# A four-layer graph, mixture and expert network on one core: the edge check moved into the mixture, node scaling into the counting, and a ring of fifteen weight tiles in the last stage

## The chip, the core and the metric

The kernel runs on 1 core of one Trainium2 chip. TensorE multiplies matrices, VectorE, ScalarE and GpSimd compute on its results, and SyncE issues most loads; 16 DMA engines move the data. The metric is device time in microseconds (us); the number that counts is the median of several executions. A profile is one further execution.

## The reference, cut to what matters

512 nodes of 768 features pass through four layers; each adds to the nodes x a graph network over 8704 edges, a linear-attention mixture, and a feed-forward stage with or without experts. Order: gnn0/mix0, ffn0, mix1/gnn1, ffn1, mix2/gnn2, ffn2, mix3/gnn3, ffn3.

```python
edge_index = jnp.stack([src, dst])
xn = _layernorm(x, axis=-1)
x = x + _L0_gnn_ref(xn, edge_index, edge_attr_256, ...)  + _L0_mix_ref(xn[None], ...)[0]
x = x + _L0_ffn_ref(_layernorm(x, axis=-1)[None], ...)[0]
...
x = x + _L3_ffn_ref(_layernorm(x, axis=-1)[None], ...)[0]
```

The last stage, 16 experts of which each takes the 64 nodes that score highest for it:

```python
scores = jax.nn.sigmoid(x @ gate_weight.T)
topk_score, topk_ids = jax.lax.top_k(scores.T, capacity)   # capacity 64
xg = x[topk_ids]
gate = jax.nn.silu(jnp.einsum('ecd,efd->ecf', xg, Wg))
up = jnp.einsum('ecd,efd->ecf', xg, Wu)
out = jnp.einsum('ecf,edf->ecd', gate * up, Wd) * topk_score[..., None]
y = jnp.zeros((n, d), x.dtype).at[topk_ids.reshape(-1)].add(out.reshape(-1, d))
shared = jax.nn.silu(hidden_states @ Ws_g.T) * (hidden_states @ Ws_u.T) @ Ws_d.T
```

## The kernel before, in words

Nodes lie as 4 blocks of 128 (NT = 4), features as 6 chunks of 128 (KC = 6). A scheduler orders instructions by the program's order and the tiles' readers and writers; `issue_after` holds an instruction behind another. Memory of a pool that is closed goes to the next one, which then waits for the old tiles' last users.

**Counting (`counts`, first 237 us).** Edges become one-hot rows (`ohd`, `so`), and matmuls (L516) count edges per pair of nodes for three or four types, packed as digits of one number. L474 sums the edge features. `digits` (L476) takes each of four blocks apart: ScalarE casts the bytes to S and R (L488, L490), GpSimd and VectorE add them up (L493 to L498) with totals kept in `total`, and GpSimd stores them. L533 to L544 then compare the totals with what they must be: a sum over VectorE (L535), a matmul with ones, and the flag `big`. If the flag is set, `counts_any` counts in another way; the test stands at L2089 (load of the flag) and L2090 (branch), behind mix0. gnn2 (L1560) loads the flag again. Nodes are normalized (`norm`) into xn, which lies where the counting's tiles lay; so its scaling (L406) waits for the end of the counting. `to_fm` turns xn into xnT by 24 transposes (L355) and six copies (L250, L252). Then mix0 starts with its v blocks (L334).

**Gates of ffn0 and ffn2 (`moe`).** The gate's weight wg is loaded on ScalarE's queue at the start of `moe`.

**End of the third mixture.** Its last projection adds the 8 blocks of 512 x 768 to x; beside it runs the rest of gnn3, whose last add to x is L1796. Each block of x that is done is normalized and stored to `there` by GpSimd (L1704). `to_fm` with `cut` turns three of four blocks early.

**Last stage (`ffn3`).** Experts go in pairs q = 0 to 7, hidden features in 8 parts n of 384: 64 steps. A step needs 4 tiles of weights up (two experts, Wg and Wu) and 2 tiles down (Wd), each 128 x 2304 floats, 1152 KB, loaded by SyncE (L258) into a ring (pool `f3_w`) of 13. The ring's pool is opened after `self.cw.close()`, so its memory holds everything that the earlier stages' weights (`wp`, 6 tiles) and bias rows (`rowp`) held, and more. At any time the up of step i + 1 (L1981) is issued ahead of the down of step i (L1997).

The start, in order: gate matmuls (L342), scores sc (L1850), then `first_rank` (L1858) for experts 0 and 1: transposes put all scores of an expert on every partition, in one bank of PSUM; per block of nodes ScalarE counts by signs (L1865), VectorE settles ties (L1868). `choose` builds one-hot rows oh (L1896), `fetch` multiplies them with the node numbers, casts `who` (L1909) and gathers the chosen rows from HBM on GpSimd's queue (L1911). `turn` transposes the rows to xg, which the first up needs. Twelve units of a shared expert (`shared`, `shared_down`, weights `sw` loaded by GpSimd, L1950, ring of 6) fill gaps by a list `beside` written per step; unit 0's two up halves stand around the first fetch. `rank` for later pairs, `way` (weights back to nodes) and `back` (adds to x) are in `beside` too.

Of the kernel before, what the change touches and what calls it, by code (L numbers as in the profile page):

```python
# [10 lines left out]
F32 = mybir.dt.float32  # L11
# [159 lines left out]
class Net:  # L171
    def __init__(self, ctx, tc, dram, at, out):
        self.tc, self.nc, self.d, self.at, self.out = tc, tc.nc, dram, at, out
        nc = self.nc
        self.cw = ExitStack()
        self.wp = self.cw.enter_context(tc.tile_pool(name="wp", bufs=6, side="right"))
        self.keep = ctx.enter_context(tc.tile_pool(name="keep", bufs=1))
        self.small = ctx.enter_context(tc.tile_pool(name="small", bufs=4))
        self.rowp = self.cw.enter_context(tc.tile_pool(name="rowp", bufs=2, side="right"))
# [87 lines left out]
    def wk(self, ap):  # L267

        return self.w(ap).rearrange("p (k n) -> p k n", k=KC)
# [87 lines left out]
    def to_fm(self, x, out, cut=0):  # L357

        if cut:
            ps = [self.ps() for _ in range(KC)]  # L360
            for t in range(cut // P):
                for f in range(KC):
                    self.tr(ps[f][:, t * P : (t + 1) * P], x[:, t, f * P : (f + 1) * P])
            for f in range(KC):
                self.copy(out[:, f, :cut], ps[f][:, :cut])
            for f in range(0, KC, 3):
                p = self.ps()
                for k in range(3):
                    self.tr(p[:, k * P : (k + 1) * P], x[:, NT - 1, (f + k) * P : (f + k + 1) * P])
                self.copy(out[:, f : f + 3, cut:], p[:, :HW].rearrange("p (k n) -> p k n", k=3))  # L370
            return
        ps = [self.ps() for _ in range(KC)]
        for t in range(NT):
            for f in range(KC):
                self.tr(ps[f][:, t * P : (t + 1) * P], x[:, t, f * P : (f + 1) * P])
        for f in range(KC):
            self.copy(out[:, f, :], ps[f])

# [16 lines left out]
    def norm1(self, x, out, t):  # L395

        nc = self.nc
        st = self.small.tile([P, 2, 6], F32, name="st")
        mv = self.small.tile([P, 2], F32, name="mv")
        r = self.small.tile([P, 1], F32, name="rs")  # L400
        for h in range(2):
            nc.vector.bn_stats(st[:, h, :], x[:, t, h * HW : (h + 1) * HW])
        nc.vector.bn_aggr(mv, st)
        self.root = nc.scalar.activation(r, mv[:, 1:2], AF.Sqrt, bias=self.eps).ins
        nc.vector.reciprocal(r, r)
        nc.vector.tensor_scalar(out[:, t, :], x[:, t, :], mv[:, 0:1], r, OP.subtract, OP.mult)  # L406
# [24 lines left out]
    def counts(self, c0, g0):  # L431
# [11 lines left out]
        after = c0.enter_context(tc.tile_pool(name="g0_t", bufs=1))  # L443
        EFT = after.tile([P, 2, N], F32, name="EFT")
        with ExitStack() as c:
# [11 lines left out]
            top = one.tile([P, 8], F32, name="top")  # L457
            total = one.tile([P, 10], F32, name="total")
# [20 lines left out]
            def digits(h, t, ps):  # L479
# [9 lines left out]
                R = dg.tile([P, 3, N], F32, name="R", bufs=1)  # L489
# [3 lines left out]
                nc.gpsimd.tensor_add(A, R[:, 0, :], R[:, 1, :])  # L493
# [12 lines left out]
            for h in range(2):  # L506
# [15 lines left out]
                for t in range(2):  # L522
                    digits(h, t, [acc[t, n] for n in range(2)])

                while len(left) > (17, 0)[h]:
                    features(left.pop(0))
            for f in range(2):
                self.copy(EFT[:, f, :], eft[f])

            three = one.tile([P, EJ], F32, name="three")  # L530
            nc.vector.tensor_scalar(three, ind[:, 3, :], 2.0, None, OP.is_le, OP.add, accum_out=total[:, 8:9])
            nc.vector.tensor_scalar(total[:, 8:9], total[:, 8:9], -1.0, float(-EJ), OP.mult, OP.add)
            nc.vector.memset(total[:, 9:10], 0.0)  # L533
            check = one.tile([P, 2], F32, name="check")
            nc.vector.tensor_reduce(check[:, 0:1], total, AX.X, OP.add)  # L535
            high = one.tile([P, 1], F32, name="high")
# [4 lines left out]
            bad = one.tile([P, 2], F32, name="bad")  # L541
# [3 lines left out]
        return AT, EFT, after  # L545
# [98 lines left out]
    def mix0(self, xnT):  # L644
# [3 lines left out]
        with ExitStack() as outer, ExitStack() as c:  # L648
# [16 lines left out]
            self.tm(d["m0_wqkv"], xs, put_v, self.bias(d["m0_bv"]), nbs=(4, 5), bias_at=2 * D)  # L665
            for g in range(2):
                qk = one.tile([97, 2, 4, N], F32, name="qk")
# [49 lines left out]
            self.project(outer, attn, "m0")  # L717
# [97 lines left out]
    def moe(self, f, act, xn, xnT, bs=None, fill=None, later=None):  # L815
# [6 lines left out]
        with ExitStack() as c:  # L822
            one = c.enter_context(tc.tile_pool(name=f + "_one", bufs=1))
            two = c.enter_context(tc.tile_pool(name=f + "_two", bufs=2))
            wg = one.tile([P, KC, 32], F32, name="wg")
            nc.scalar.dma_start(wg.rearrange("p k e -> p (k e)"), d[f + "_wg"])
# [732 lines left out]
    def gnn2(self, xn, xnT):  # L1559
        big = self.nc.values_load(self.big[:1], min_val=0, max_val=1)  # L1560
        with self.tc.If(big > 0) as cmp:
# [252 lines left out]
    def ffn3(self, xnT, gate, there):  # L1814
# [5 lines left out]
        with ExitStack() as c:  # L1820
            two = c.enter_context(tc.tile_pool(name="f3_two", bufs=2))
            one = c.enter_context(tc.tile_pool(name="f3_one", bufs=1))
            sp = c.enter_context(tc.tile_pool(name="f3_s", bufs=6))

            self.cw.close()
            self.wp = c.enter_context(tc.tile_pool(name="f3_w", bufs=13))

            first = self.small.tile([P, 1], F32, name="r3")
            with self.tc.issue_after(self.root):
                nc.scalar.activation(first, self.eps, AF.Sigmoid)  # L1830
            io = one.tile([P, P], F32, name="io")
            nc.gpsimd.iota(io, pattern=[[1, P]], base=0, channel_multiplier=0, allow_small_or_imprecise_dtypes=True)
            number = self.number
            above = one.tile([P, NT, NX], F32, name="above")
            counted = one.tile([P, NX, NT, 3], F32, name="counted")
# [5 lines left out]
            side = one.tile([P, 7 * P], BF16, name="side")  # L1841
# [4 lines left out]
            loT = one.tile([P, N], F32, name="loT")  # L1846
# [12 lines left out]
            def first_rank(e):  # L1859
                p = self.ps()  # L1860
                for t in range(NT):
                    self.tr(p[:, t * P : (t + 1) * P], sc[:, t, e : e + 1].to_broadcast([P, P]))
                for t in range(NT):
                    junk = one.tile([P, N], BF16, name="sign")
                    i = nc.scalar.activation(junk, p, AF.Sign, scale=BIGGER, bias=low[:, t, e : e + 1],  # L1865
                                             accum_out=signs[:, t, e : e + 1])
                    junk = one.tile([P, N], BF16, name="junk")
                    nc.vector.scalar_tensor_tensor(junk, p, sc[:, t, e : e + 1], side[:, (3 - t) * P : (7 - t) * P],  # L1868
                                                   OP.is_equal, OP.mult, accum_out=sides[:, t, e : e + 1])
                return i  # L1870

            def rank(e):
# [4 lines left out]
                for t in range(NT):  # L1877
                    s = sc[:, t, e : e + 1]
                    for n, (a, b, op) in enumerate(((0, t * P, OP.is_ge), (t * P, N, OP.is_gt))):
                        if a < b:  # L1880
                            junk = one.tile([P, N], BF16, name="junk")
                            nc.vector.tensor_scalar(junk[:, a:b], p[:, a:b], s, None, op, OP.add,
                                                    accum_out=counted[:, e, t, n : n + 1])
                    junk = one.tile([P, N], BF16, name="junk")
                    nc.vector.scalar_tensor_tensor(junk[:, :P], p[:, t * P : (t + 1) * P], s, before, OP.is_equal, OP.mult,
                                                   accum_out=counted[:, e, t, 2:3])
                nc.vector.tensor_reduce(above[:, :, e : e + 1], counted[:, e], AX.X, OP.add)
# [3 lines left out]
            def choose(q):  # L1891

                oh = two.tile([P, NT, 2, CAP], BF16, name="oh")
                chosen[q] = oh, two.tile([P, KC, P], F32, name="xg")
# [4 lines left out]
            rows = {}  # L1899

            def fetch(q):
# [4 lines left out]
                sums = two.tile([P, 1], F32, name="sums")  # L1906
                nc.vector.tensor_reduce(sums, p[:, :2], AX.X, OP.add)
                who = two.tile([P, 1], I32, name="who")
                nc.vector.tensor_copy(who, sums)  # L1909
                rows[q] = two.tile([P, D], F32, name="rows", bufs=1)  # L1910
                nc.gpsimd.indirect_dma_start(out=rows[q], out_offset=None, in_=there,  # L1911
                                             in_offset=bass.IndirectOffsetOnAxis(ap=who, axis=0))
                return i
# [10 lines left out]
            def way(q):  # L1924

                oh = chosen[q][0]
                os = two.tile([P, NT, 2, CAP], F32, name="os", bufs=1)
                nc.vector.tensor_mul(os, oh, sc[:, :, 2 * q : 2 * q + 2, None].to_broadcast([P, NT, 2, CAP]))
                ways[q] = two.tile([P, N], F32, name="ohT")
# [15 lines left out]
            def shared(u, b):  # L1945
                if b == 0:
                    hs[u] = [two.tile([P, N], F32, name="hs")]
# [6 lines left out]
                i = self.acc(p, [(w[:, k, :], xnT[:, k, :]) for k in range(KC)])  # L1954
                h = hs[u][0]
                if b == 0:
# [12 lines left out]
            def up_w(q, n):  # L1969
                return [[self.wk(d[w][2 * q + a, n]) for a in range(2)] for w in ("f3_Wg", "f3_Wu")]  # L1970

            def down_w(q, n):
                return [self.wr(d["f3_Wd"][2 * q + a, n]) for a in range(2)]

            def up(q, n, ws):
# [7 lines left out]
                h = two.tile([P, HW], F32, name="h")  # L1983
# [4 lines left out]
            def down(q, n, h, wd, po):  # L1988
# [3 lines left out]
                hT = two.tile([P, HW], F32, name="hT")  # L1992
# [18 lines left out]
            for q in range(8):  # L2011
                beside[8 * q + 2].append((way, q))
# [8 lines left out]
            rest = pieces[2:]  # L2021
# [3 lines left out]
            for e in range(2):  # L2025
                last = first_rank(e)
            nc.vector.tensor_scalar(signs, signs, 0.5, float(N // 2), OP.mult, OP.add)
            nc.vector.tensor_add(above[:, :, :2], signs, sides)
            with tc.issue_after(last.ins):
                last = shared(0, 0)  # L2030
            choose(0)

            with tc.issue_after(last.ins):
                last = fetch(0)
            with tc.issue_after(last.ins):
                shared(0, 1)
            turn(0)
            held = up(*steps[0], up_w(*steps[0]))
            for i, (q, n) in enumerate(steps):
# [9 lines left out]
                if n == 7:  # L2049
                    outs[q] = two.tile([P, D], F32, name="outs")  # L2050
# [11 lines left out]
def tile_net(ctx, tc, dram, at, out, only=ALL):  # L2062
# [10 lines left out]
    with ExitStack() as ck, ExitStack() as c0:  # L2073
        g0 = c0.enter_context(tc.tile_pool(name="g0", bufs=1))
        if "counts" in only:
            AT, EFT, g0_t = net.counts(c0, g0)
# [82 lines left out]
```

## Time and profile before

| | us |
|---|---|
| median of 3 executions (4174.07 to 4178.53) | 4176.57 |
| profiled execution | 4179.75 |
| its span | 4177.7 |
| TensorE busy in the span | 4027.0 (96%) |
| VectorE, ScalarE, GpSimd busy | 1214.8, 648.5, 274.4 |
| DMA moved | 710.89 MB, mean 170 GB/s |
| ring weights of the last stage | 384 loads of 1152.0 KB, 22.2 from issue to landing |
| mean granted TensorE clock | 0.989 |

Rows of the profile give an engine, the line of the code, the operation, output and inputs by the program's names, and a count; idle time of the engine just ahead stands in brackets, with what ended it. PEld is TensorE's loading of weights. The slices divide the span in 40 equal parts of 104 us; digits are tenths busy. A wait is given as the engine and line waiting, what it waited for, the time in total, how often, and the longest.

### The profile page before, as it was taken

Reading aid. Unit: us, or ns where it says so; the run is one execution under the profiler, and the core shown is the slowest. Engines: PE = TensorE matmul, PEld = TensorE weight load, DVE = VectorE, ACT = ScalarE, POOL = GpSimd, SP = SyncE. Lnnn points to the kernel's source line nnn. Section 1 sums busy time; section 2 is a strip of 40 time slices with the busy share of each in tenths; the row PEclk is TensorE's granted clock in tenths of the full one; section 3 lists DMA queues with packets and bytes.
Section 4 is the critical chain, followed back from the end, with each engine's and each line's share of the span. In section 5 each row is a group of like instructions: output and inputs, shape, how many; then the busy total and the mean of one; then the engine's idle time right before and its main releaser. Section 6 shows DMA issues by size and latency. Waiting matters only on the chain. (4 is left out here: it accounts for less than half of the span.)

```text
span 4177.7 us, 39229 instructions
## 1 busy us (share of the span) xinstructions
PE 4027.0 (96%) x16020; PEld 2066.7 (49%) x16061; DVE 1214.8 (29%) x2899; ACT 648.5 (16%) x1222; POOL 274.4 (7%) x329
## 2 busy tenths in 40 slices
PE   8989999999999999999999999999989999999998
PEld 3444555554455667655544444454644444444443
DVE  7721211113332147313411111126832122212211
ACT  1212000012222216311101010024510000000000
POOL 1120000010031010000000000020200000000000
PEclk9999999999999999999999999999999999999999
DMA  3210011121184011302211111082099999999998
GB/s 124 71 69 34 35 63 51 53 78 36 62 312 143 23 70 46 132 25 78 98 46 57 46 61 42 3 325 82 15 373 422 421 421 421 421 422 421 422 422 361
DMA packets 99548, 710.89 MB, mean 170 GB/s; under 512 B 12608, under 2 KB 12944, under 8 KB 29984
## 3 DMA queue, kind: packets, MB, share of 16 engines
q1 hardware_dynamic: 78064, 601.20, 36.0%
q0 software_dynamic: 16816, 95.80, 6.1%
q10 hardware_dynamic: 4480, 11.28, 0.7%
q8 instruction: 131, 2.15, 0.2%
q14 instruction: 57, 0.47, 0.0%
HBM read 685.68 MB, written 22.54 MB: 170 GB/s over the span
## 5 line engine op out<-in xcount | busy, mean ns | idle before, releaser
L1981 PE MATMUL ps<-w,xg 128*64 128x384 f32 x3072 | 567.6, 489 | 5.3 <-DMA w<-in_f_Wg_dram 3.0
L1981 PEld LDWEIGHTS ps<-w,xg 128*64 128x64 f32 x3072 | 235.3, 137 | 293.1 <-issue 264.1
L1601 PE MATMUL ps<-aT,w 128*128 128x512 f32 x864 | 372.3, 592 | 0.0
L1997 PE MATMUL ps<-w,hT 128*64 128x384 f32 x1536 | 322.5, 490 | 6.3 <-DMA w<-in_f_Wd_dram 2.9
L334 PE MATMUL ps<-xnT,w 128*128 128x512 f32 (+1 forms) x732 | 322.8, 598 | 0.2 <-ACT xnT L252 0.2
L1601 PEld LDWEIGHTS ps<-aT,w 128*128 128x128 f32 x864 | 164.2, 190 | 203.6 <-issue 202.3
L334 PE MATMUL ps<-w,xnT 128*128 128x384 f32 x672 | 222.7, 488 | 0.0
L334 PEld LDWEIGHTS ps<-xnT,w 128*128 128x128 f32 (+1 forms) x732 | 134.7, 185 | 176.3 <-issue 172.7
L1997 PEld LDWEIGHTS ps<-w,hT 128*64 128x64 f32 x1536 | 132.5, 136 | 171.8 <-issue 146.5
L411 DVE TENSOR_TENSOR x<-x,ps 128x384 f32<-128x384 f32 x224 | 123.4, 553 | 263.7 <-PE ps L334 193.0
L334 PE MATMUL ps<-C,parts 128*128 128x512 bf16 x843 | 187.8, 380 | 3.5 <-DVE inv L1623 2.4
L334 PE MATMUL ps<-w,hT 128*128 128x384 f32 x552 | 184.6, 490 | 2.6 <-ACTq L1056 1.7
L334 PEld LDWEIGHTS ps<-w,xnT 128*128 128x128 f32 x672 | 127.7, 191 | 88.8 <-issue 5.8
L1611 DVE TENSOR_TENSOR aT<-inv,ps 128x512 f32<-128x512 f32 x72 | 49.4, 686 | 365.7 <-PE ps L334 365.7
L1984 ACT ACTIVATE h<-ps 128x384 f32<-128x384 f32 x64 | 31.4, 490 | 788.9 <-PE ps L1981 788.9
L516 PE MATMUL ps<-ohd,so 128*128 128x512 bf16 x533 | 128.4, 391 | 21.1 <-DVE so L513 20.4
L1985 DVE TENSOR_TENSOR h<-h,ps 128x384 f32<-128x384 f32 x64 | 35.4, 554 | 376.8 <-PE ps L1981 376.8
L334 PEld LDWEIGHTS ps<-w,hT 128*128 128x128 f32 x552 | 103.1, 190 | 80.1 <-ACT xbT L252 7.1
L334 PE MATMUL ps<-w,aT 128*128 128x384 f32 (+1 forms) x416 | 139.6, 486 | 0.5 <-DVE aT L250 0.4
L334 PE MATMUL ps<-xnT,sw 128*128 128x512 f32 x288 | 139.6, 616 | 0.0
L334 PEld LDWEIGHTS <-parts 128*128 128x128 bf16 x864 | 84.8, 98 | 108.1 <-issue 8.9
L334 PE MATMUL ps<-w,nodesT 128*128 128x384 f32 x384 | 129.1, 486 | 0.0
(507 smaller groups left out, 4634.7 us busy)
## 6 DMA issues: line engine op xcount, KB each, us to landing
w<-in_f_Wg_dram SPq DMA_DIRECT2D x128, 1152.0 KB, 22.2
w<-in_f_Wu_dram SPq DMA_DIRECT2D x128, 1152.0 KB, 22.2
w<-in_f_Wd_dram SPq DMA_DIRECT2D x128, 1152.0 KB, 22.2
w<-in_g_w_dram SPq DMA_DIRECT2D x54, 1152.0 KB, 5.2
w<-in_m_wqkv_dram SPq DMA_DIRECT2D x24, 1152.0 KB, 7.5
w<-in_g_t_dram SPq DMA_DIRECT2D x12, 1152.0 KB, 5.1
w<-in_m_wp_dram SPq DMA_DIRECT2D x8, 1152.0 KB, 5.1
ea<-in_edge_attr_dram SPq DMA_DIRECT2D x34, 256.0 KB, 2.7
```

The source lines that it names most:

```text
L334: i = self.nc.tensor.matmul(out, a, b, start=n == 0, stop=n == len(pairs) - 1)
L411: self.nc.vector.tensor_add(xs, xs, p)
L516: nc.tensor.matmul(p, so[:, n, t * P : (t + 1) * P], ohd[:, j, :], start=j == 0, stop=j == EJ - 1)
L1601: nc.tensor.matmul(outs[nb * 3 + f], w[:, k, f * P : (f + 1) * P], xT[:, k, :], start=first and k == 0, stop=last and k == KC - 1)
L1611: nc.vector.tensor_mul(aT[:, f, :], inv[:, r, :], p)
L1981: nc.tensor.matmul(p[a * 64 : a * 64 + 64, :HW], xg[:, k, a * CAP : (a + 1) * CAP], ws[b][a][:, k, :], start=k == 0, stop=k == KC - 1)
L1984: nc.scalar.activation(h, pg[:, :HW], AF.Silu)
L1985: nc.vector.tensor_mul(h, h, pu[:, :HW])
L1997: nc.tensor.matmul(po[nb][a * 64 : a * 64 + 64, :HW], hT[:, f * P + a * 64 : f * P + a * 64 + 64], wd[a][:, f, nb * HW : (nb + 1) * HW], s ...
```

## The change

- **Counting.** Small totals lie in a tile of their own for the whole kernel (`edge`). xn gets memory on the other side of the pools, and `norm` is called inside the counting. The check becomes a function `checked`, called in mix0 behind the v blocks; the flag is loaded once, ahead of mix0's second group (`self.wrong`), for both tests. R is kept in BF16. Some bias loads are held behind the first half's adds (`self.after`).
- **Gates.** `gate_of` loads the gate weights on GpSimd's queue into the caller's pool.
- **`to_fm_last`** replaces `to_fm` with `cut`: which engine copies what is fixed; the sigmoid's table load stands behind the last copy.
- **ffn3.** The ring has 15 tiles: six of `wp` (indices 0 to 3, 9, 10), five of `early`, two of `tail`, two of `rest_`, in the places of earlier tiles, so that each waits for its own place. All tiles of the ring start on multiples of 512 bytes. Several tiles are single-buffered or share a tag (`outs`, `os`, `h`, hT, hs, ohT); sw has 5 buffers. `first_ranks` uses two banks: ScalarE works on one expert while VectorE works on the other. `who` is cast by the reduction. shared(0, 1) is split around the first fetch, and `shared_down` of unit 0 comes ahead of the rows' transposes.

```diff
-    def to_fm(self, x, out, cut=0):
...
+    def gate_of(self, pool, f):
+        t = pool.tile([P, KC, 32], F32, name=f + "_gate")
+        self.nc.gpsimd.dma_start(t.rearrange("p k e -> p (k e)"), self.d[f])
+        return t
...
+    def to_fm_last(self, x, out):
+
+        nc, cut = self.nc, (NT - 1) * P
+        ps = [self.ps() for _ in range(KC)]
+        for t in range(NT - 1):
+            for f in range(KC):
+                self.tr(ps[f][:, t * P : (t + 1) * P], x[:, t, f * P : (f + 1) * P])
+        for f in (0, 1, 3, 4):
+            i = nc.scalar.copy(out[:, f, :cut], ps[f][:, :cut])
+        with self.tc.issue_after(self.scaled):
+            for f in (2, 5):
+                nc.vector.tensor_copy(out[:, f, :cut], ps[f][:, :cut])
...
-                R = dg.tile([P, 3, N], F32, name="R", bufs=1)
+
+                R = dg.tile([P, 3, N], BF16, name="R", bufs=1)
...
+        def checked():
+
             nc.vector.tensor_reduce(check[:, 0:1], total, AX.X, OP.add)
-            high = one.tile([P, 1], F32, name="high")
             nc.vector.tensor_reduce(high, top, AX.X, OP.max)
             nc.vector.tensor_scalar(check[:, 1:2], high, 2.0 ** 24, None, OP.is_ge)
             p = self.ps()
             self.acc(p[:, :2], [(self.ones, check)])
-            bad = one.tile([P, 2], F32, name="bad")
             nc.vector.tensor_scalar(bad, p[:, :2], 0.0, None, OP.not_equal)
...
-            self.tm(d["m0_wqkv"], xs, put_v, self.bias(d["m0_bv"]), nbs=(4, 5), bias_at=2 * D)
+            with tc.issue_after(self.after):
+                bv = self.bias(d["m0_bv"])
+            self.tm(d["m0_wqkv"], xs, put_v, bv, nbs=(4, 5), bias_at=2 * D)
+            checked()
             for g in range(2):
+                if g:
+                    self.wrong = nc.values_load(self.big[:1], min_val=0, max_val=1)
...
-            wg = one.tile([P, KC, 32], F32, name="wg")
-            nc.scalar.dma_start(wg.rearrange("p k e -> p (k e)"), d[f + "_wg"])
...
-            sp = c.enter_context(tc.tile_pool(name="f3_s", bufs=6))
-
-            self.cw.close()
-            self.wp = c.enter_context(tc.tile_pool(name="f3_w", bufs=13))
+            tail = c.enter_context(tc.tile_pool(name="f3_m", bufs=2))
+            sp = c.enter_context(tc.tile_pool(name="f3_s", bufs=5))
+            c.callback(self.cw.close)
+            early = c.enter_context(tc.tile_pool(name="f3_w", bufs=5))
+            self.cr.close()
+            rest_ = c.enter_context(tc.tile_pool(name="f3_r", bufs=2))
+            self.taken = 0
+
+            def ring():
+                i, self.taken = self.taken % 15, self.taken + 1
+                return self.wp if i < 4 or 9 <= i < 11 else early if i < 9 else tail if i < 13 else rest_
...
+            def first_ranks():
+
+                ps = [self.ps() for _ in range(2)]
+                for e in range(2):
+                    for t in range(NT):
+                        self.tr(ps[e][:, t * P : (t + 1) * P], sc[:, t, e : e + 1].to_broadcast([P, P]))
+                for e in range(2):
+                    for t in range(NT):
+                        junk = two.tile([P, N], BF16, tag="h", name="sign")
+                        i = nc.scalar.activation(junk, ps[e], AF.Sign, scale=BIGGER, bias=low[:, t, e : e + 1],
+                                                 accum_out=signs[:, t, e : e + 1])
+                    for t in range(NT):
+                        junk = one.tile([P, N], BF16, name="junk")
+                        j = nc.vector.scalar_tensor_tensor(
+                            junk, ps[1 - e], sc[:, t, 1 - e : 2 - e], side[:, (3 - t) * P : (7 - t) * P],
+                            OP.is_equal, OP.mult, accum_out=sides[:, t, 1 - e : 2 - e])
+                return i, j
...
-                hT = two.tile([P, HW], F32, name="hT")
+                hT = two.tile([P, HW], F32, name="hT", bufs=1)
...
-            rest = pieces[2:]
+            rest = pieces[4:]
...
+            last, _ = first_ranks()
             nc.vector.tensor_scalar(signs, signs, 0.5, float(N // 2), OP.mult, OP.add)
             nc.vector.tensor_add(above[:, :, :2], signs, sides)
+
             with tc.issue_after(last.ins):
                 last = shared(0, 0)
             choose(0)
-
             with tc.issue_after(last.ins):
-                last = fetch(0)
+                last = shared(0, 1, lambda: fetch(0))
             with tc.issue_after(last.ins):
-                shared(0, 1)
+                for t in range(NT):
+                    shared_down(0, t)
             turn(0)
...
         if "counts" in only:
-            AT, EFT, g0_t = net.counts(c0, g0)
...
+            right = ExitStack()
+            xn = right.enter_context(tc.tile_pool(name="L0n", bufs=1, side="right")).tile([P, NT, D], F32, name="xn")
+            AT, EFT, g0_t, checked = net.counts(c0, g0)
+            with tc.issue_after(net.begun[0]), tc.issue_after(net.begun[1]):
+                net.constants()
+                net.norm(net.x, xn)
...
-                wrong = nc.values_load(net.big[:1], min_val=0, max_val=1)
-                with tc.If(wrong > 0):
+                with tc.If(net.wrong > 0):
```

## The prediction on record

> **What bounds the kernel now.** I read the slices of the span first, then a table by stage, then the timeline of the two places where TensorE stands still, and last the waits and the chain.
>
> ```profile
> PE   8989999999999999999999999999989999999998
> DMA  3210011121184011302211111082099999999998
> GB/s 124 71 69 34 35 63 51 53 78 36 62 312 143 23 70 46 132 25 78 98 46 57 46 61 42 3 325 82 15 373 422 421 421 421 421 422 421 422 422 361
> ```
>
> TensorE is busy nearly everywhere, so time falls only where it pauses or where it waits for bytes. DMA is at nine tenths in the last eleven slices alone: that is the last stage (ffn3). The slice before it moves almost nothing (15 GB/s). By stage (PE, PEld, DVE, ACT, POOL busy, granted clock, DMA share, GB/s):
>
> ```profile
> 2950.00:3000.00 50.00, 49.83 (x265) 34.30 (x264) 46.96 (x78) 30.17 (x48) 15.56 (x11) 1.00 0.00 1
> 3000.00:3050.00 50.00, 48.36 (x239) 32.70 (x238) 29.11 (x64) 15.37 (x27) 10.69 (x20) 1.00 0.31 110
> 3050.00:3100.00 50.00, 40.33 (x185) 18.80 (x185) 18.23 (x59) 10.16 (x23) 2.15 (x3) 0.90 1.01 418
> 3100.00:3200.00 100.00, 99.26 (x512) 44.34 (x512) 19.25 (x53) 5.97 (x13) 3.17 (x5) 1.00 1.01 421
> ```
>
> The DMA engines idle until 3043.68, when the first ring weight is issued, and are then full. The queue's own waits say why: ring issues (L258) stand behind the release of the whole area.
>
> ```profile
> SPq L258 <- DVE x L1796: 128.0, 1, 128.0
> ```
>
> From 3043.68 to the last landing at 4164.03 the stream runs 1120.35 us without a pause; 384 weight tiles go by in pairs 5.57 us apart (2.787 each). The chain ends on it, so near its end the stage is bound by bytes:
>
> ```profile
> 4141.79 22.19 DMA w<-in_f_Wd_dram
> 4163.98 0.04 issue
> 4164.03 4.08 PE ps L1997 x20
> ```
>
> But all of TensorE's waits for weights come in 4124–4164 and sum to only about 8 us. Both limits lie close together: that caps what earlier loads can bring.
>
> TensorE's own pauses at the start of that stage, and in front of the first mixture:
>
> ```profile
> 3043.45 2.13 PE L355 MATMUL ps<-ident,xn 128*128 128x128 f32 x18
> 3052.80 5.32 PE L334 MATMUL ps<-xnT,sw 128*128 128x512 f32 x12
> 3065.43 0.75 PE L334 MATMUL ps<-number,oh 128*128 128x2 bf16 x4 [7.31 <-issue]
> 3066.04 8.20 PE L334 MATMUL ps<-xnT,sw 128*128 128x512 f32 x12
> 3075.92 2.48 PE L1981 MATMUL ps<-w,xg 128*64 128x384 f32 x14 [0.32 <-DVE xg L250]
> ```
>
> ```profile
> 245.25 0.56 PE L334 MATMUL ps<-check,ones 128*128 128x2 f32 x2 [7.81 <-DVE check L535]
> 246.42 2.52 DVE L406 TENSOR_SCALAR xn<-x,mv,rs 128x768 f32<-128x768 f32 x4
> 247.24 5.27 PE L355 MATMUL ps<-ident,xn 128*128 128x128 f32 x24 [1.43 <-DVE xn L406]
> 252.36 0.88 PE L334 MATMUL ps<-w,xnT 128*128 128x384 f32 x2
> ```
>
> Brackets give idle time and what ended it.
>
> **Part 1: check and normalization.** TensorE ends counting at 237.44, idles 7.81 until the check's total is there, spends 0.56, idles 1.43 until xn is scaled, transposes, and starts the projection at 252.36. In the change xn has its own place, its four scalings (2.52 us) stand within the counting, and the check comes after the v blocks. In the built order the transposes directly follow the last counting matmul and wait for nothing new. VectorE has room for 2.52 us: it is 65% busy in 60–160 and 62% in 160–237, where TensorE is 95–97% busy; uncovered they'd cost at most those 2.5.
>
> How long will the transposes take? Here 24 took 5.27 us (0.220 each) at a granted clock of 0.50, after the idle stretch; at 3043.45, straight behind matmuls, 18 took 2.13 (0.118 each) at 1.00. The Trainium skill, "TensorE: Matmul & The Clock Gate", Part 4, says that full clock does not engage for transposes, since they don't count as activity the same way. By that, 5.27 stays; by the row, 24 × 0.118 = 2.84. I take the row: transposes behind busy work keep the clock here. They run 237.5–240.3, and the projection starts about 0.4 us after (the first copy is 0.6): 240.7. That is 252.36 − 240.7 = 11.6 early (9.2 by the rule). The check's matmuls return between v and qk: −0.56. Result 11.0.
>
> What is now late? The check's reduction stands on VectorE before the first v copy, behind ScalarE's S copy (waiting for a store until 241.36) and GpSimd's sums: it ended at 245.10, the v copy is due at about 245, and one such copy comes each 8 us with several banks free. Even 3 us late is covered; without cover it costs those 3. No pause over 1.2 us between 252 and 700 except the branch, so the gain isn't given back. GpSimd's stores and bias steps are only reordered. R in BF16 changes GpSimd casts nobody on the path awaits: 0.
>
> **The branch.** At the test (L2090) TensorE stands 6.16 us. The flag is now read earlier, once. But VectorE's compare-and-branch starts at 484.1, right after its last add, and its release comes at 489.5: the time is behind the branch, which stays. I take 0 (bounds −0.5 to +2 gained).
>
> **Part 2: gate weights.** In ffn0 the first gate matmul waited:
>
> ```profile
> 1160.24 2.77 PE L342 MATMUL ps<-xnT,wg 128*32 128x512 f32 x10 [2.20 <-DMA wg<-in_f_wg_dram]
> ```
>
> Loaded early from GpSimd's queue, it starts when the first copy is done (1158.2), and its last input is ready at 1159.4: 1.9 gained (1 to 2.2). GpSimd's issue of about 0.5 us has whole stages as cover. In ffn2 no such wait is seen: 0.
>
> **Part 3: start of the last stage.** Now 8 sign/compare pairs alternate on one bank, ScalarE (0.69) waiting for VectorE (0.75) and back: 3052.57 to 3064.71, 12.1 us. With two banks crossed, both run at once: 8 × 0.75 plus gaps ≈ 6.5, ending near 3059.2; the sums 0.3, then oh 0.91: 3060.4. TensorE does shared(0,0) to 3058.1 and half of shared(0,1) to 3060.8 (5.32/2), with no pause and so none of the slower clock that made the second block 8.20 instead of 5.32. Then number·oh, who, and the gather is issued near 3061.7. It landed 7.48 later with DMA full; now the ring is full and DMA nearly idle, so I take 3.5 (2 to 7.5). Under it go the other half (to 3064), its product on VectorE (0.6) and eight shared-down products (5.4, brought forward; at the very end eight products of that shape take 5.37): 3070.2. The rows' transposes (0.9) and copies (0.6) follow: first up at 3072.0, 3.9 earlier, with 5.4 of later work done. TensorE alone would then end 3.9 + 5.4 + the 8 of weight waits = 17.3 earlier: the cap.
>
> **Part 4: the ring.** Fifteen tiles, nine or ten of them loaded in the idle stretch before 3043, the rest by 3060. The bytes left are 369 tiles, but DMA restarts only when TensorE frees the first pair, half an up step (4 us) on: 3076.0. Before, the stream of 1120.35 held 384 × 2.787 = 1070.2, 38 smaller loads (30 shared weights, 8 gathers, 0.393 MB at 422 GB/s = 0.93) = 35.4, and 14.7 of first latency and gaps. After: 369 × 2.787 = 1028.4, 37 × 0.93 = 34.4, 14.7: 1077.5. So the last landing is 4153.5, against 4164.03: 10.5 earlier. Early slots come in pairs while the queue is nearly empty, worth 0 to 5 us of stall; fully overlapped first latency gives back up to 3. Range 6 to 13, at most 17.3. I keep 10.5. TensorE's wait thus becomes an earlier one for the same weights.
>
> **Alignment.** The ring tiles now start on multiples of 512 bytes; they lay at 448 past one. "DMA: Bandwidth & Descriptors", section "How a descriptor splits into AXI transactions", says that a descriptor not starting on 256 bytes pays for the unused bytes ahead: at 192 past, 6 beats on 288, 2%. That would be 2% of 1028 = 20 us and leave TensorE's cap. The trace disagrees: by its packets, 6144 bytes into tiles 160 past such a boundary (ffn0) and into aligned ones (ffn2) both take 234 ns. I take 0, keeping the other as a rival.
>
> Other edits (single buffers for hT, hs, outs and ohT; five shared-weight buffers; smaller counters): the earlier reader stands ahead in TensorE's order by at least a step (12 us), which hides them. A shared weight waiting on GpSimd has only later gathers behind it. Late sigmoid table load (1.28): beside TensorE's transposes. 0 each; without cover some 0.6 per step for hT.
>
> **Sum.** 11.0 + 1.9 + 10.5 = 23.4. The profiled execution took 4179.75 (span 4177.7 and 2.05 around); the median is 3.2 below it. 4176.57 − 23.4 = 4153.2; I say 4153.
>
> **Rivals.**
> - *Aligned packets are faster (0.16).* Last stage 17.3: total 30.2, 4146. For: the page. Against: equal packets here.
> - *The front gain doesn't arrive (0.10).* The scalings delay the counting or v copies wait behind the check. Part 1 gives 1–2: total 14, 4162. Against: VectorE's free third.
> - *The change doesn't do what it says: the ring starts no earlier in effect (0.09).* Slots of the earlier stage free late or early stalls are long. Part 4 gives nothing or 3: total 14, 4162.
> - *Slower (0.07).* Fifteen tiles on one alignment make DMA writes and TensorE's reads of the ring collide, so the pace falls. For: packets of 9216 bytes take 347 ns with TensorE on other tiles, 352 on average in this stage. Against: matmuls there take 489 ns, as elsewhere. The gain of 23.4 is used up at 2.787 + 23.4/369 = 2.850 a tile (+2.3%); at 2.88 it costs 34 and gives 4187.
>
> **Numbers.** The likeliest case has 0.58. A measurement here resolves about 0.2%, 8.4 us. The range takes the first rival's end with the branch's bound (4144) up to the two partial cases with small shares (4167). Faster 0.87, same 0.06 (both partial cases together), slower 0.07.
>
> **What would show it.** Transposes at 237.5 in about 2.9 us; no gate wait in ffn0; DMA traffic of ring weights before 3030 in the span; the first up 17 us earlier in the span (3059); pairs still 5.57 apart; last landing 23 earlier. A pace of 2.73 shows the first rival; 2.85 the last. If TensorE waits for weights already before 3200, the ring is the step that failed.

## The result, and the profile after

The changed kernel takes 4129.25 us (median, 4128.16 to 4130.86); before took 4177.55 in the same comparison. The ratio is 0.9884, 95% interval 0.9871 to 0.9897: 48 us faster. I had forecast 4153, at best 4144: the sign was right, the size half of what came.

The slices of the changed kernel's span (TensorE's and DMA's busy tenths, and the bytes moved):

```profile
PE   8999999999999999999999999989999999999999
DMA  3210111121183020301211111073189999999998
GB/s 128 72 68 35 47 58 46 69 68 44 55 330 117 24 92 35 134 33 71 99 35 69 39 64 46 3 295 117 47 343 427 427 428 427 427 427 427 427 427 362
```

The last stage streams at 427 GB/s where before showed 421 to 422: the pace itself changed. By stage (PE, PEld, DVE, ACT, POOL busy, clock, DMA share, GB/s):

```profile
2950.00:3000.00 50.00, 50.00 (x275) 35.97 (x274) 39.52 (x80) 26.54 (x41) 6.90 (x8) 1.00 0.07 24
3000.00:3050.00 50.00, 46.75 (x187) 26.15 (x187) 26.48 (x64) 13.17 (x32) 9.22 (x18) 1.00 0.89 362
3050.00:3100.00 50.00, 49.26 (x258) 21.47 (x254) 16.47 (x60) 3.04 (x6) 2.07 (x3) 1.00 0.93 373
3100.00:3200.00 100.00, 99.92 (x541) 47.75 (x538) 19.35 (x49) 6.41 (x13) 1.63 (x3) 1.00 1.01 427
```

DMA already runs ahead of the stage, which now begins at 3020. From TensorE's timeline at its start:

```profile
3020.20 2.13 PE L359 MATMUL ps<-ident,xn 128*128 128x128 f32 x18
3029.01 7.89 PE L2004 MATMUL ps<-xnT,sw 128*128 128x512 f32 x18
3036.74 0.40 PE L338 MATMUL ps<-number,oh 128*128 128x2 bf16 x4
3040.67 5.43 PE L338 MATMUL ps<-sw,hs 128*128 128x384 f32 x16 [0.85 <-DVE hs L2011]
3047.21 7.96 PE L2033 MATMUL ps<-w,xg 128*64 128x384 f32 x48 [0.46 <-DVE xg L254]
```

The 7.31 pause and the slow shared block are gone. And the front, where the transposes stand straight behind the last counting matmul:

```profile
230.49 3.05 PE L359 MATMUL ps<-ident,xn 128*128 128x128 f32 x24
233.83 4.11 PE L338 MATMUL ps<-w,xnT 128*128 128x384 f32 x12 [0.29 <-ACT xnT L256]
```

Where the 50.0 us up to the last matmul went in the two profiles, read from the starts of TensorE's instructions (in us):

| stretch | before | after | gained |
|---|---|---|---|
| to the last counting matmul | 237.1 | 230.1 | 7.0 |
| from there to mix0's first matmul | 15.3 | 3.8 | 11.5 |
| mix0, to the first matmul behind the branch | 237.3 | 237.7 | -0.4 |
| to ffn0's gate | 670.6 | 668.8 | 1.8 |
| to the last stage's gate | 1887.8 | 1883.9 | 3.9 |
| last stage, gate to first up | 27.9 | 23.0 | 4.9 |
| first up to the last matmul | 1097.1 | 1075.8 | 21.3 |
| from there to the end of the span | 4.7 | 6.0 | -1.4 |

The fifth row can't be put down to the change: it varies by as much from run to run. Two runs of before with edits elsewhere (below) took 1878.4 and 1878.5 for it, and the runs of the changed code 1876.0 to 1883.9; why is not known. Times below are therefore compared by stretch, and totals by medians. "The stage" below is the last stage from the start of its gate to the start of the last matmul: 1125.0 before, 1098.8 now.

### The profile page after: what moved, and what is told of

Read it like the earlier page. It is cut to its first block, busy times and chain, and to the rows that moved or that the text cites. A ratio compares the mean times of both kernels' runs of the same rounds, so it can differ in the third digit from the quotient of the medians.

```text
span 4129.1 us, 39273 instructions
## 1 busy us (share of the span) xinstructions
PE 4010.7 (97%) x16061; PEld 2063.3 (50%) x16061; DVE 1211.0 (29%) x2890; ACT 648.4 (16%) x1223; POOL 275.0 (7%) x330
```

## Experiments: the pace of the stream

**All fifteen tiles off the boundary.**

```diff
-        self.edge = edge.tile([P, 120], F32, name="edge")
+        self.edge = edge.tile([P, 136], F32, name="edge")
...
-            one.tile([P, 16], F32, name="room")
```

> The changed kernel with all fifteen ring tiles (and the shared weights) starting 448 bytes past a multiple of 512, as the ring of before lay; nothing else differs. Theory (start addresses set the pace of the weight stream): pairs of weights 5.57 apart again instead of 5.47, 369 x 0.05 = 18 more, about 4147. Rival (fifteen tiles and their early loads make the gain, addresses do nothing): pairs stay at 5.47, about 4129.

Measured: median 4139.5, ratio 0.992 (0.9906 to 0.9933), so about 15 lost against the changed kernel's ratio. The stage takes 1112.5 instead of 1098.8. SyncE issues each pair of weights 5.57 behind the last one in this run (first fence) and 5.47 in the changed kernel (second):

```profile
4060.87 3.11 SPq L262 DMA_DIRECT2D w<-in_f_Wg_dram  x2
4066.43 3.11 SPq L262 DMA_DIRECT2D w<-in_f_Wu_dram  x2
4072.01 4.40 SPq L262 DMA_DIRECT2D w<-in_f_Wd_dram  x2
```

```profile
4056.05 3.05 SPq L262 DMA_DIRECT2D w<-in_f_Wg_dram  x2
4061.51 3.06 SPq L262 DMA_DIRECT2D w<-in_f_Wu_dram  x2
4066.99 3.06 SPq L262 DMA_DIRECT2D w<-in_f_Wd_dram  x2
```

With fifteen tiles the stream has the pace of before's thirteen again, so it is the address that sets it and not the count of tiles. The expected 18 were not reached: the stage lost 13.7.

**Nine tiles at 256 past it.**

```diff
-            above = one.tile([P, NT, NX], F32, name="above")
+            above = self.edge[:, 32:96].rearrange("p (t x) -> p t x", x=NX)
```

> The changed kernel with nine of the fifteen ring tiles, and the shared weights, starting 256 bytes past a multiple of 512; six stay on multiples of 512. Theory 256 (a start on 256 bytes is enough, as the rule on splitting descriptors has it): pairs 5.47, about 4129. Theory 512 (only multiples of 512 run at the fast pace): nine fifteenths of the loss of the run with all at 448, about 4140.

Measured: median 4123.63, ratio 0.9882 (0.9866 to 0.9897), the stage 1099.5, pairs 5.47 apart: as the changed kernel. 256 is enough. That agrees with the Trainium skill, "DMA: Bandwidth & Descriptors", section "How a descriptor splits into AXI transactions", which speaks of bytes read; here it is the place that a load writes to. The estimate from its beats, 6 on 288 or 2.1%, is a little high: pairs are 1.8% further apart (5.57 against 5.47), and the stage as a whole moves 421 instead of 427 GB/s, 1.4%.

**The kernel before, on the boundary.**

```diff
+            one.tile([P, 16], F32, name="room")
             above = one.tile([P, NT, NX], F32, name="above")
```

> The kernel before, its thirteen ring tiles and shared weights moved by 64 bytes to multiples of 512; nothing else differs. Theory (addresses set the pace): pairs 5.47 instead of 5.57, 384 x 0.05 = 19 less for the stream; if TensorE's own work allows it, about 4158. The cap of my prediction (TensorE has only 8 us of waits for weights to lose in that stage) would give 4169. Rival (addresses do nothing): 4177.

Measured: median 4159.9, ratio 0.9971 (0.9959 to 0.9983), so 12 to 14 less than before beside it, by the ratio and by the medians (4173.85). The stage falls from 1125.0 to 1113.0, with no other edit. This row of the stage, of the run on the boundary, has TensorE full and the stream at the new rate:

```profile
3500.00:3600.00 100.00, 100.00 (x503) 45.43 (x502) 21.24 (x57) 5.55 (x11) 2.63 (x4) 1.00 1.01 427
```

That lies between the 19 of the theory and the 8 of my cap, which did not hold: the stage became 12.0 shorter. TensorE does the same work in nearly the same order in both runs, so they can be laid side by side from the first up. For about 790 us they agree to 0.01 us; then before falls back, by 1.2 until 870 and by 11.7 until the last matmul. So before, TensorE's own work set the pace for most of the stage and the stream only its end. On the boundary TensorE waits for no ring weight at all. The 8 us were also read too low: the profile counts a wait from the modelled end of a matmul, and where it shows 1.49 idle, the starts are 1.98 apart instead of the usual 0.265. That leaves out 0.22 for each of nine waits, 2.0 in all, and 1.8 of the 11.7 stay unexplained.

## Experiments: the early loads and the start of the stage

**Only the first load held.**

```diff
+            self.gate, self.before = self.ended, 0
             held = up(*steps[0], up_w(*steps[0]))
```

Here `self.ended` is the third mixture's last matmul.

> The changed kernel with its first ring load held until the last matmul of the third mixture's projection is done, so that nothing of the ring is loaded in the idle stretch ahead; fifteen aligned tiles as before. The recorded sum (earlier loads end the stream earlier: 10.5): about 10 slower than the changed kernel. Theory now (on aligned tiles the stream has slack and TensorE's own work sets the end, as in the run of before on 512): 0 to 4 slower.

Measured: median 4127.23, ratio 0.9884 (0.9868 to 0.9901), the stage 1098.8. Nothing lost, but the edit did less than it says: the scheduler put the held load behind five others, which went out from 2994.41 on. So this run only says that five tiles ahead are as good as nine.

**All fifteen held.**

```diff
+        if getattr(self, "late", 0):
+            self.late -= 1
+            self.tc.add_manual_dep(i.ins, self.ended.name, ...)
...
+            self.late = 15
             held = up(*steps[0], up_w(*steps[0]))
```

> The changed kernel with every one of the first fifteen ring loads held until the third mixture's last matmul (the run before held only the first load, and five others went out ahead). Aligned tiles. Theory (TensorE is the bound on aligned tiles, 1076 from first up to end): within 3 of the changed kernel. The recorded sum (loads in the idle stretch end the stream 10.5 earlier): about 10 slower.

Measured: median 4137.7, ratio 0.991 (0.9896 to 0.9923); the stage 1111.2, 12.4 more. The theory I had formed, that TensorE alone bounds the stage once tiles are aligned, falls; the recorded 10.5 for early loads was about right. This run's chain runs through weights that each take 22 us from issue to landing, as before's did:

```profile
4072.40 21.97 DMA w<-in_f_Wu_dram
4094.37 0.02 issue
4094.39 0.02 SPq L262
4094.40 0.03 issue
4094.43 21.97 DMA w<-in_f_Wd_dram
```

The changed kernel's chain has such a piece too, so the chain alone doesn't part the two. TensorE's waits for ring weights do: 8.6 here, 2.5 in the changed kernel.

**Both: late, and off the boundary.** The edits of the run just above and of the one with all fifteen tiles off the boundary, together.

> The changed kernel with both: all ring tiles 448 bytes past a multiple of 512, and the first fifteen loads held until the third mixture is done. Theory (on these addresses bytes are the bound, so there the early loads count): first up to end longer than the 1089.5 of the run with early loads, by 2 to 10. Rival (early loads are worth nothing in either case): 1089.5.

Measured: median 4154.37, ratio 0.9949 (0.9936 to 0.9963). First up to last matmul 1103.5, 14.0 above 1089.5 where 2 to 10 were expected; the stage 1126.6. The four runs make a square (the stage, the changed kernel's code otherwise; in brackets TensorE's waits for ring weights):

| | 448 past | on 512 | gained by the address |
|---|---|---|---|
| loads held | 1126.6 (18.6) | 1111.2 (8.6) | 15.4 |
| loads early | 1112.5 (12.4) | 1098.8 (2.5) | 13.7 |
| gained by early loads | 14.1 | 12.4 | |

Each gain shows with the other or without it, and the two nearly add up. The upper left corner is as long as the kernel before (1125.0), although its first up comes 4.9 earlier and shared work is moved forward. Its first ring load goes out 3.8 ahead of the gate, before's 4.3: where the stream starts no earlier and decides when the stage ends, an earlier start of TensorE is worth nothing.

**Ranks in turn, as before.**

```diff
                 for e in range(2):
+                    p = self.ps()
                     for t in range(NT):
-                        i = nc.scalar.activation(junk, ps[e], AF.Sign, ...)
+                        i = nc.scalar.activation(junk, p, AF.Sign, ...)
...
+                        j = nc.vector.scalar_tensor_tensor(junk, p, sc[:, t, e : e + 1], ...)
```

> The changed kernel with the two first rankings one after the other, ScalarE and VectorE taking turns on one bank, as before. Theory (TensorE is the bound of the last stage, so a later first up is a later end): ranks 12 us instead of 6.5, TensorE pauses some 4 to 6 before the first fetch, 4 to 6 slower than the changed kernel. Rival (DMA is the bound and the ring refills meanwhile): within 2 of it.

Measured: median 4135.43, ratio 0.9905 (0.9888 to 0.9921); the changed kernel beside it 4129.0. The stage is 1107.0, 7.8 more than the 1099.2 beside it. TensorE's pause and the slower clock behind it are back in this run:

```profile
3039.29 0.75 PE L338 MATMUL ps<-number,oh 128*128 128x2 bf16 x4 [4.74 <-issue]
3039.90 5.24 PE L2002 MATMUL ps<-xnT,sw 128*128 128x512 f32 x6
```

From the first up to the last matmul the changed kernel takes 1076.2 beside it, this run 1076.3: with the loads early, a later first up is a later end.

## Experiments: the front

**The check first again.**

```diff
+            checked()
         with tc.tile_pool(name="L0", bufs=1) as pool:
...
-            checked()
             for g in range(2):
```

> The changed kernel with the edge check ahead of the first transposes again instead of behind the v blocks. xn is scaled within the counting as now. Theory (the wait for the check was the pause, and the lower clock after it slows the transposes): TensorE idles 7 to 8 ahead of the check's matmul, 24 transposes take about 5 instead of 3, 10 to 12 slower than the changed kernel. Rival (the rule that transposes never run at full clock, so only the pause comes back): 24 transposes take 5 in both.

Measured: median 4135.73, ratio 0.9902 (0.9885 to 0.9918), 6.7 above the median beside it, where 10 to 12 were expected. In the profiles mix0 starts 11.0 later; the profiled execution was the slowest of its four (4143.1), and why the medians are less far apart isn't settled. TensorE in this run (first), and in the changed kernel beside it:

```profile
237.99 0.56 PE L338 MATMUL ps<-edge,ones 128*128 128x2 f32 x2 [7.86 <-DVE edge L560]
238.41 5.27 PE L359 MATMUL ps<-ident,xn 128*128 128x128 f32 x24
```

```profile
229.40 2.78 PE L359 MATMUL ps<-ident,xn 128*128 128x128 f32 x24
232.47 4.11 PE L338 MATMUL ps<-w,xnT 128*128 128x384 f32 x12 [0.29 <-ACT xnT L256]
```

The same 24 transposes take 5.27 us at a granted clock of about 0.5 behind the pause, 2.78 at 1.00 without it. The rule cited in the prediction, that full clock doesn't engage for transposes, doesn't hold for these 24; the row was the better guide.

**Bias steps at the start again.**

```diff
-            with tc.issue_after(self.after):
-                bv = self.bias(d["m0_bv"])
+            bv = self.bias(d["m0_bv"])
```

and the same for `self.project(outer, attn, "m0")`.

> The changed kernel with the first mixture's bias steps on GpSimd no longer held behind the first half's adds, so that they run at the start of the counting as before. Theory (GpSimd's bias steps stretch VectorE's one-hot instructions while TensorE has no backlog): TensorE pauses again between 13 and 27 us in the span, counting ends about 7 later, about 4136. Rival (the counting became shorter through BF16 sums or moved totals): counting ends at 230.5 as now, about 4129.

Measured: median 4129.58, ratio 0.9902 (0.9887 to 0.9917). The interval doesn't part it from the changed kernel, and the median is the rival's 4129. The profile speaks for the theory, with less than its 7: TensorE has the pauses again (3.70, 0.48 and 0.88 between 18 and 28 us), and the last counting matmul starts at 234.2 against 229.2 to 230.1, 4 to 5 later.

**Before, with that one edit.**

```diff
+            with tc.issue_after(self.after):
+                bv = self.bias(d["m0_bv"])
```

and the same for `self.project(outer, attn, "m0")`.

> The kernel before with one edit: the first mixture's bias steps on GpSimd are held behind the first half's adds. Theory (they stretch VectorE's one-hot instructions while TensorE has no backlog): no pause of TensorE between 13 and 27 us, counting ends 5 earlier, about 5 less than before. Rival (the other edits of the counting did it): within 1 of before.

Measured: median 4166.39, ratio 0.9984 (0.9975 to 0.9993), about 7 less than before where 5 were expected; the last counting matmul starts at 228.4 instead of 237.1. TensorE in the first 40 us of before, then of this run:

```profile
13.24 3.90 PE L516 MATMUL ps<-ohd,so 128*128 128x512 bf16 x9 [13.24 <-DVE so L513]
17.53 0.82 PE L516 MATMUL ps<-ohd,so 128*128 128x512 bf16 x3 [0.38 <-DVE so L513]
19.94 0.40 PE L516 MATMUL ps<-ohd,so 128*128 128x512 bf16 x1 [1.59 <-DVE so L513]
21.64 3.17 PE L516 MATMUL ps<-ohd,so 128*128 128x512 bf16 x7 [1.30 <-DVE so L513]
26.57 8.10 PE L516 MATMUL ps<-ohd,so 128*128 128x512 bf16 x28 [1.76 <-DVE so L513]
```

```profile
12.01 11.89 PE L516 MATMUL ps<-ohd,so 128*128 128x512 bf16 x48 [12.01 <-DVE so L513]
23.74 2.75 PE L474 MATMUL ps<-ohd,part 128*128 128x512 bf16 x11
```

The same 48 matmuls take 21.3 us in before and 11.7 here. The four pauses are 5.0 of that. The rest is mostly the clock: behind the pauses, from 20.2 to 30.4, before is granted 0.50, and its matmuls start 0.43 apart instead of 0.22; here the clock is at 1.00 from 14.8 on.

And VectorE and GpSimd in before at that place:

```profile
13.99 0.91 POOL L291 CAST bias<-row 1x768 bf16<-1x768 f32 x1 [0.16 <-DMA row<-in_m_bv_dram]
14.13 0.92 DVE L510 TENSOR_SCALAR ohd<-io,ind 128x512 bf16<-128x512 int16 x1
14.97 2.50 DVE L513 TENSOR_SCALAR so<-io,ind,worth 128x256 bf16<-128x256 int16 x2
14.98 1.63 POOL L292 TENSOR_TENSOR row<-row,bias 1x768 f32<-1x768 f32 x1
```

Elsewhere L510 takes 0.34 and a pair of L513 0.59. All ten that are stretched in the first 27 us end 0.08 to 0.15 after the end of a GpSimd instruction that they lie over: VectorE's goes on when GpSimd's is done. The Trainium skill, "SBUF — State Buffer", section "Who interferes with whom", says as much: VectorE's tensor_scalar in its fast modes and GpSimd hold one port pair in turn, for a whole instruction (which mode these run in, no view here shows). At the start TensorE has no backlog, so such a turn can become a pause. Moved behind the first half the bias steps cost it next to nothing: from 60 us to the end of the counting it idles 7.1 in before and 7.4 in this run.

**The changed kernel once more**, beside three of these runs (only the first load held, ranks in turn, the check first).

> The changed kernel itself, beside the next three on one chip, as their baseline. The ratio to before should be 0.988 again.

Measured: median 4129.0, ratio 0.9889 (0.9873 to 0.9906).

## Why the prediction fell short, step by step

- **Part 1, check, scaling, transposes: right.** Forecast 11.6 less 0.56; measured 11.5 and -0.4. The transposes took 3.05 where 2.84 was worked out.
- **Part 1, "GpSimd's stores and bias steps are only reordered": wrong.** Costed at 0; the counting became 7.0 shorter, and the bias edit alone gave before about 7. I had seen that TensorE waits 20.4 us for VectorE in the counting, and not asked what made VectorE late, nor what the pauses do to the clock. What the counting's other edits add isn't settled: undoing the bias edit in the changed kernel gave back 4 to 5 of the 7.
- **The branch: right at 0.** The pause is 6.43 now, 6.16 before.
- **Part 2, gate weights: right.** Forecast 1.9; that stretch gained 1.8.
- **Part 3, start: right in kind.** Forecast 3.9, measured 4.9 from gate to first up.
- **Part 4, the ring: right in kind, near in size.** Forecast 10.5 for start and early loads; off the boundary they are worth 12.5 (1125.0 to 1112.5).
- **"Alignment: I take 0": wrong.** It is worth 13.7 in the changed kernel. I set packet times from ffn0 and ffn2 against the page's rule: single packets took 234 ns on both kinds of address. In those stages, which don't fill the DMA engines, this row didn't show what the address costs in the full one. The prediction had a nearer row and read it for another rival, as a collision with TensorE's reads: packets of 9216 bytes take 352 ns on average in the full stage, 347 elsewhere. On the boundary, with TensorE reading as before, they take 348 there.
- **The cap of 17.3: wrong in all three terms.** The stage gained 26.2. The earlier first up is 4.9 and not 3.9. The waits for weights that before could lose are 11.7 and not 8, as the run of before on the boundary shows. And from the first up to the last matmul the changed kernel takes 9.6 less than that run (1085.4 to 1075.8), where 5.4 of moved work was counted; what the other 4.2 are isn't settled. The rival "aligned packets are faster" named the right mechanism and was cut off by this cap.

In sum: the forecast 23.4, and 7.0 for the counting, 13.7 for the addresses, 2.0 for early loads and start (12.5 against 10.5), and 3.9 from the stretch that varies by itself: 50.0. Of these 1.4 go back behind the last matmul, where the changed kernel's profile shows 6.0 and most of the other runs 4.7 or 4.8. The two effects that the forecast put at nothing, addresses and counting, make 20.7 together.

## What to carry to other kernels

Where a stage streams at full rate, start its DMA buffers on multiples of 256 bytes, and judge it by the interval between pairs of loads in the full stage, not by single packets elsewhere. Where an engine is awaited, look at what else runs in that moment: small GpSimd steps moved out of a start without backlog were worth about 7 us here. When bytes and TensorE lie close together, test the edits in a square: here early loads and addresses each gained 12 to 15, with the other or without it. TensorE's earlier start counted with both of them and was worth nothing with neither.

## What was not expected of the hardware

Loads into tiles 448 bytes past a multiple of 512 come 1.8% further apart (a pair in 5.57 instead of 5.47 us) in a stage with DMA full; 256 past is as good as 0. VectorE's one-hot instructions of about 0.34 us grow to as much as 1.79 while GpSimd works on a single row of 768, and behind the pauses that this made TensorE's granted clock was 0.50 for 10 us. 24 transposes take 5.27 or 2.78 us, with a pause of 8 us ahead or without.
